# The order of a two-layer graph kernel's transfers: all of one queue in program order, an input loaded into its own tile, additions split and a count moved

## The chip, the cores and the metric

The kernel runs on one core of a Trainium2 chip. The metric is the device time of one execution in microseconds (us), of which the median over several executions is given. Five engines work in parallel, each through its own stream of instructions: TensorE (PE, matrix products into PSUM), VectorE (DVE), ScalarE (ACT), GpSimd (POOL) and SyncE (SP), which here issues nearly all transfers between the memories.

## The reference

For each of 32 items x (512 nodes of 512 features) and one adjacency matrix, two layers are computed, each with its input added back and normalized:

```python
def _L0_gnn_ref(x, adj, Wq, bq, Wk, bk, Wv, bv):
    H, HD = (8, 64)
    q, k, v = ((x @ W + b).reshape(b_, n, H, HD) for W, b in ...)
    scores = einsum('bihd,bjhd->bhij', q, k) / sqrt(HD)
    scores = scores + where(adj == 0, -1e9, 0.0)[None, None, :, :]
    return einsum('bhij,bjhd->bihd', softmax(scores), v).reshape(b_, n, H * HD)

def _L1_gnn_ref(x, adj, weight, bias):
    deg_inv_sqrt = where(adj.sum(1) > 0, rsqrt(adj.sum(1)), 0.0)
    norm_adj = adj * deg_inv_sqrt[:, None] * deg_inv_sqrt[None, :]
    return einsum('nm,bmo->bno', norm_adj, einsum('bni,io->bno', x, weight)) + bias

x = _layernorm(x + _L0_gnn_ref(x, adj, Wq, bq, Wk, bk, Wv, bv))
x = _layernorm(x + _L1_gnn_ref(x, adj, weight, bias))
```

## The kernel before

The items run one after the other in a loop over b (32 of them), with the work of three items interleaved: while attention of item b runs, the keys, queries and values of b + 1 are computed, the graph convolution of b - 1, and the last normalization and the stores of b - 2. An item has two halves. Each half begins with `stretch` (L526) for two of the four groups of heads: scores, exponentials, their sums, and the products with the values. Then follows a run of products on PE, with smaller work of the other engines put at chosen places between them: `play` (L106) takes a list of PE steps and a table "after step n do these". In the first half the PE steps are the keys and queries of b + 1 (L435), in the second the convolution and the values of b + 1 (L379). The products are multiplied out by a seven-product scheme (`seven`, L357), so that PE's steps come in groups of eight matrix products, whose PSUM regions are copied by ACT ("put") or added by DVE ("add"). A region is written again by a later step only when it has been read.

The order on PE, DVE, ACT and POOL is the program's: `InOrder` (L35) wraps these four engines, and each operation goes through `keep_in_program_order` (L45). The transfers issued through SP are not wrapped: `nc.sync.dma_start` leaves it to the framework's scheduler where in SP's stream each is put. SP issues its stream in order. In the program as built, SP's stream in the first item is: eight copies yT<-yb, the store of w1's parts, the load of the values' weights, the store of `fourth`, four copies yT<-yb, two loads of x, four copies, six loads of x, the load of the queries' weights. In later items the four residual loads and the four stores of results stand alternately after the first eight copies yT<-yb, and the x loads stand two before and six after the last four such copies.

The transfers and their tiles:

- `load_x` (L123): x of one item, in two halves of four transfers, rearranged for a transpose by DVE (`turn`, L131; in the trace xT<-e). It fills the last two of the eight buffers of exponentials (`NUM`, in the trace e). In the loop it is called in the second half of item b for item b + 2.
- `load_residual` (L181): x again, in natural order, into the tile xr, for the addition after attention; `gather` (L191), an accumulating transfer that POOL issues, adds the values' bias to it.
- `unload_values` (L507): DVE transposes the product of a head group into yb, a tile with one buffer, and SP copies it in four transfers to yT (L521). The next group's transpose waits for these.
- `swap` (L263): loads the values' weights or the queries' weights, in the form prepared for the seven-product scheme, into one tile wqv that both use in turn.
- `fourth` (L964): in the first item POOL computes one more combination of the values' weights (`weigh_values`), which is stored to the prepared weights in memory (L967). The tile has the tag "lo", one of the places that tiles of several names share one after the other.
- `store` (L840): ACT applies the last normalization, and the result goes out (L850). For most items it lies in the tile y, which has the tag "lo" too, as has `lo` (L677), the low part of the layer's input that DVE computes for the next item.

At the end there is no next item. In the item before the last, the second half's table runs to step 22; then `stretch` of the last item is called with a list `late` to be done between its two groups (L902): the last two `low` and the four `lift` (L682), which add the second layer's bias to yT, on POOL for the item before the last. In the last item's first half the PE steps are the convolution of the item before. After the loop, the last item's own convolution runs alone; `judge` and `count` sum up a check that the fast path was exact (its result decides whether a general version runs), and `measure` takes the statistics for the normalizations.

Of the kernel before, what the change touches and what calls it, by code (L numbers as in the profile page):

```python
# [10 lines left out]
F32 = mybir.dt.float32  # L11
# [7 lines left out]
P = 128  # L19
# [31 lines left out]
def unshifted(  # L51
# [21 lines left out]
    LAST = B - 1  # L73
    tensor, vector, scalar, gpsimd = (InOrder(tc, e) for e in (nc.tensor, nc.vector, nc.scalar, nc.gpsimd))

# [23 lines left out]
    def each(f, *args):  # L99
        return [lambda a=a: f(*a) if isinstance(a, tuple) else f(a) for a in args]  # L100
# [12 lines left out]
    X = {}  # L113
# [8 lines left out]

    def load_x(b, j):  # L123
        X[b, j] = NUM[:, 6 + j].rearrange("p k (n t r) -> p (k n) t r", t=DT, r=32)
        for q in range(4):
            nc.sync.dma_start(
                X[b, j][32 * q : 32 * (q + 1)],
                x[b, ts(j, HALF), ts(q, P)].rearrange("(k s) (t r) -> s k t r", s=32, r=32),
            )
# [51 lines left out]
    def load_residual(b):  # L181
        if b < LAST:
            t = acts.tile([P, NT, D], F32, name="xr", tag="zT", bufs=1)
        else:
            t = wk[:, 3:].rearrange("p k u o -> p k (u o)")
        R[b] = [t[:, i, :] for i in range(NT)]
        for i in range(NT):
            nc.sync.dma_start(R[b][i], x[b, ts(i, P), :])  # L188
        return [lambda: gather(t, rows(bv))]
# [73 lines left out]
    def swap(k):  # L263
        nc.sync.dma_start(wqv, stored[k])
    load_x(1, 0)
# [241 lines left out]
    def unload_values(b, g, av):  # L507
        if b == LAST and g == ORDER[-1]:
            t = work.tile([P, N], F32, name="avT", tag="yb", bufs=1)
            scalar.copy(t[:, :HALF], av[:, :HALF])  # L510
            vector.tensor_copy(t[:, HALF:], av[:, HALF:])
            AV[b, g] = t
            return
        yb = work.tile([P, 4, NT, 32], F32, name="yb", bufs=1)
        vector.transpose(
            yb.rearrange("p l i s -> p i l s"), av.rearrange("p (i r l) -> p i l r", i=NT, l=4)
        )
        if g == ORDER[0]:
            YT[b] = acts.tile([P, NT, D], F32, name="yT")
        for q in range(4):  # L520
            nc.sync.dma_start(  # L521
                YT[b][:, :, (4 * g + q) * 32 : (4 * g + q + 1) * 32],
                yb[32 * q : 32 * (q + 1)],
            )
# [181 lines left out]
    def convolve(b):  # L706
# [135 lines left out]
        def store(n, at):  # L842
            y = row(n)
            rstd, add = (a[:, n - at : n - at + 1] for a in t[at])
            if last and n == 1:
                vector.tensor_scalar(y, y, rstd, add, op0=ALU.mult, op1=ALU.add)
                scalar.dma_start(out[b, ts(n, P), :], y)
                return
            scalar.activation(y, y, AF.Identity, bias=add, scale=rstd)
            nc.sync.dma_start(out[b, ts(n, P), :], y)  # L850

# [43 lines left out]
    for b in range(B):  # L895
# [3 lines left out]
        if b == LAST - 1:  # L899
            nc.sync.dma_start(w1[:, 1:5, 0, P:], stored[2][:, 1:5, 0, P:])  # L900
        biased = []
        late = ahead["low"][2:] + ahead["lift"] if b == LAST else []  # L902
        stretch(b, one, late + back["measure"][:3] if back else ())
# [12 lines left out]
        if b < LAST:  # L916
            k0, k1 = keys_and_queries(b + 1, 0), keys_and_queries(b + 1, 1)
            main = [p for pair in zip(k0, k1) for p in pair]
            if b == 0:
                exact = each(compare, *range(NT))  # L920
                weights = each(lambda k: weigh_part(w1, gpsimd, k), *range(4))
# [17 lines left out]
            if b == 0:  # L939
                nc.sync.dma_start(stored[2], w1)  # L940
        else:
            e = f[b]
            conv = c[b - 1]
            play(conv["first"], {
                0: rest + store[:1] + conv["parts"][:0], 1: store[1:2] + ahead["judge"] + conv["parts"][:1],
                2: store[2:] + e["sums0"],
# [8 lines left out]
        turn0, turn1, combined = turns()  # L955
        if b + 2 < B:
            load_x(b + 2, 0)
            load_x(b + 2, 1)
        if b < LAST:
            end = f[b]  # L960
            if b == 0:
                fourth = acts.tile([P, 4, P], F32, name="fourth", tag="lo", bufs=1)

                def weigh_values():  # L964
                    for k in range(4):
                        weigh_quarter(wqv, wv_quarters, k, gpsimd, fourth)
                    nc.sync.dma_start(stored[1][:, 1:5, 0, P:], fourth)  # L967
                    weigh_quarter(w1, w1_quarters, 3, gpsimd)
# [4 lines left out]
            else:  # L973
# [21 lines left out]
                else:  # L995
# [5 lines left out]
                        15: measure[:1], 16: measure[1:2], 17: measure[2:3], 18: measure[3:] + end["root"],  # L1001
                        19: norm[:1], 20: norm[1:2] + low[:1], 21: norm[2:3] + low[1:2] + biased, 22: norm[3:],
                    }
# [18 lines left out]
    s, tail, halves = e["second"], held["measure"][2:] + held["root"] + held["store"], e["halves"]  # L1022
    run(s[:2] + halves[0] + s[2:4] + end["judge"] + held["measure"][:2])
    vector.tensor_reduce(count, FINE, AX.X, ALU.add)
    run(s[4:5] + tail[:3] + s[5:6])

# [290 lines left out]
```

## Time and profile before

| | us |
|---|---|
| median of 3 runs | 2732.19 (2731.54 to 2735.86) |
| profiled execution, its own time | 2733.05 |
| its span, first to last instruction | 2731.3 |
| mean granted PE clock | 0.996 of full speed |

The profile is that of one execution. In the page's table of transfers (their size in KB, median us from issue to landing) those that the change touches are:

```profile
yT<-yb SPq DMA_DIRECT2D x508, 64.0 KB, 2.4
e<-in_x_dram SPq DMA_DIRECT2D x248, 128.0 KB, 2.6
xr<-in_x_dram SPq DMA_DIRECT2D x122, 256.0 KB, 4.6
...
out_dram<-y SPq DMA_DIRECT2D x120, 256.0 KB, 4.8
```

SPq is SP's queue; x508 is how often. The names are the program's tiles, destination first; e stands for all eight buffers of NUM. Since four engines are wrapped by one helper, the page gives line 45 for almost all of their instructions, and one tells them apart by their tiles. SP's transfers keep their own lines.

### The profile page before, as it was taken

What the parts mean: (1) busy time and instruction counts of PE and PEld (TensorE: products, weight loads), DVE (VectorE), ACT (ScalarE), POOL (GpSimd) and SP (SyncE); (2) the same over time, 40 slices, a digit from 0 to 9 for tenths busy, and PEclk for the clock granted to TensorE, in tenths of its full rate; (3) what the DMA queues carried; (4) which work ended last, traced back from release to release, by engine and by line L of the source; (5) the groups of instructions that cost most, each with busy time, mean ns of one, the idle gap of its engine ahead of it and who ended that gap; (6) DMA issues with size and microseconds to landing.
All of it is one profiled execution on the core that took longest, in us unless ns stands there. A gap on an engine that the chain in (4) does not pass through costs nothing.

```text
span 2731.3 us, 39221 instructions
## 1 busy us (share of the span) xinstructions
PE 2693.9 (99%) x13956; PEld 1913.8 (70%) x13956; DVE 1955.1 (72%) x2743; ACT 1521.9 (56%) x2825; POOL 2051.8 (75%) x1380
## 2 busy tenths in 40 slices
PE   9899999999999999999999999999999999999997
PEld 6576776766767767767667677676676776766764
DVE  4677777677676777776776777777677767777777
ACT  4355555565555655555555556555555555565554
POOL 4577787777887777877778777778777787777764
PEclk9999999999999999999999999999999999999999
DMA  6335444454445454454544454544545444545441
GB/s 186 111 89 135 118 102 130 110 140 124 104 116 130 113 133 116 103 132 110 141 123 106 115 128 117 129 108 107 139 105 147 117 109 115 118 130 128 126 86 49
DMA packets 421996, 324.06 MB, mean 119 GB/s; under 512 B 279840, under 2 KB 348448, under 8 KB 413600
## 3 DMA queue, kind: packets, MB, share of 16 engines
q1 hardware_dynamic: 388048, 255.14, 31.9%
q0 software_dynamic: 32736, 65.02, 15.0%
q8 instruction: 113, 1.85, 0.3%
q10 hardware_dynamic: 1008, 1.31, 0.2%
q14 instruction: 91, 0.75, 0.1%
HBM read 248.78 MB, written 39.32 MB: 105 GB/s over the span
## 4 chain that ended last, share of the span: by engine, by line
PE 89%; POOL 3%; DVE 3%; DMA 2%; SPq 1%; issue 1%; ACT 1%; DVEq 0%; POOLq 0%; ACTq 0%
PE mm L45 58%; PE sc L45 16%; PE av L45 15%; DMA out_dram<-y 2%; POOL yT L45 1%; POOL acc L45 1%; DVE st L45 0%; SPq L188 0%; DVE ve L45 0%; SPq L521 0%; DVE lo L45 0%; DMA yT<-yb 0%; ACT e L45 0%; SPq L850 0%; POOL y L45 0%
## 5 line engine op out<-in xcount | busy, mean ns | idle before, releaser
L45 ACT ACTIVATE e<-e 128x1024 f32<-128x1024 f32 x512 | 540.5, 1057 | 115.9 <-DVE e L45 85.4
L45 POOL TENSOR_TENSOR acc<-acc,e 128x1024 f32<-128x1024 f32 x248 | 588.7, 2374 | 19.4
L45 DVE SCALAR_TENSOR_TENSOR e<-sc,maskT 128x1024 f32<-128x1024 f32 x512 | 585.0, 1214 | 24.0 <-PE sc L45 23.6
L45 PE MATMUL mm<-xT,wk 128*128 128x256 f32 x1792 | 464.3, 381 | 2.4 <-DVE kq L45 2.0
L45 PE MATMUL mm<-xT,wqv 128*128 128x256 f32 x1792 | 459.9, 379 | 0.0
L45 PE MATMUL sc<-kq 64*128 64x512 f32 x2048 | 458.3, 597 | 0.8 <-ACT zT L45 0.8
L45 PE MATMUL av<-e,v 128*64 128x512 f32 x2048 | 453.6, 595 | 0.1
L45 POOL TENSOR_TENSOR xT<-xT 128x512 f32<-128x512 f32 x246 | 327.2, 1340 | 102.9 <-DVE xT L45 70.7
L45 POOL TENSOR_TENSOR acc<-e 128x1024 f32<-128x1024 f32 x126 | 297.0, 2357 | 134.4 <-ACT e L45 134.4
L45 PEld LDWEIGHTS mm<-xT,wk 128*128 128x128 f32 x1792 | 336.6, 190 | 75.9 <-DVE mv L45 23.5
L45 ACT ACTIVATE kq<-mm,bias 128x256 f32<-128x256 f32 x512 | 214.2, 472 | 294.7 <-PE mm L45 288.6
L45 PEld LDWEIGHTS mm<-xT,wqv 128*128 128x128 f32 x1792 | 340.5, 190 | 46.3
L45 POOL TENSOR_TENSOR e<-e 128x512 f32<-128x512 f32 x240 | 303.7, 1276 | 72.5 <-ACT e L45 57.5
L45 PEld LDWEIGHTS sc<-kq 64*128 64x128 f32 x2048 | 192.8, 187 | 234.6 <-issue 177.0
L45 PEld LDWEIGHTS av<-e,v 128*64 128x64 f32 x2048 | 144.7, 137 | 301.4 <-issue 234.4
L45 PE MATMUL mm<-wqv,xT 128*128 128x256 f32 (+1 forms) x1736 | 306.3, 323 | 11.3 <-DVE v L45 11.3
L45 PE MATMUL mm<-w,e 128*128 128x128 f32 (+1 forms) x1680 | 297.9, 323 | 0.2 <-DVE y L45 0.2
L45 PEld LDWEIGHTS mm<-wqv,xT 128*128 128x128 f32 x1736 | 265.1, 192 | 33.6 <-DVE v L45 11.7
L45 DVE STREAM_TRANSPOSE yb<-av 128x512 f32<-128x512 f32 x127 | 91.0, 717 | 273.1 <-DMA yT<-yb 177.1
L45 PEld LDWEIGHTS mm<-w,e 128*128 128x128 f32 x1680 | 253.4, 191 | 25.3 <-DVE y L45 7.5
L45 DVE TENSOR_TENSOR v<-v,mm 128x512 f32<-128x512 f32 x217 | 146.1, 686 | 151.3 <-ACT v L45 76.5
L45 ACT ACTIVATE yT<-yT,inv 128x64 f32<-128x64 f32 x960 | 238.9, 337 | 0.0
(142 smaller groups left out, 3429.9 us busy)
## 6 DMA issues: line engine op xcount, KB each, us to landing
wqv<-wv_parts SPq DMA_DIRECT2D x31, 1792.0 KB, 8.9
wqv<-wq_parts SPq DMA_DIRECT2D x30, 1792.0 KB, 10.2
yT<-yb SPq DMA_DIRECT2D x508, 64.0 KB, 2.4
e<-in_x_dram SPq DMA_DIRECT2D x248, 128.0 KB, 2.6
xr<-in_L_gnn_bv_dram POOLq DMA_DIRECT2D x31, 1024.0 KB, 11.2
xr<-in_x_dram SPq DMA_DIRECT2D x122, 256.0 KB, 4.6
yT<-in_L_gnn_bias_dram POOLq DMA_DIRECT2D x30, 1024.0 KB, 12.3
out_dram<-y SPq DMA_DIRECT2D x120, 256.0 KB, 4.8
```

The source lines that it names most:

```text
L45: return self.tc.keep_in_program_order(op(*args, **kwargs))
```

## The change

Five edits are made together.

1. SP is wrapped like the other engines: all transfers issued through it in the loop, x's, the residual's, the weights', the copies to yT, the stores of results, are issued in the program's order. (In the changed kernel they have line 45 too.)
2. x of the third item (index 2) is loaded in the first half of the first item instead of the second, into a tile of its own, x2, with the tag "lo". `load_x` takes the tile as an argument. The loop's other calls, for later items, stay.
3. `fourth` gets the tag "hi" instead of "lo".
4. Of the four additions of the bias before the last item (`lift`), two move from the gap in the last item's first stretch to the end of the item before, after step 22; the other two move to the last item's first half, after its first step, behind the square roots of the result's normalization.
5. After the loop, the first two measurements of the item before the last come after the check's count and after the fifth step's additions, instead of before the count.

```diff
@@ -71,7 +71,9 @@
     HALF = N // 2
     ORDER = (0, 2, 1, 3)
     LAST = B - 1
-    tensor, vector, scalar, gpsimd = (InOrder(tc, e) for e in (nc.tensor, nc.vector, nc.scalar, nc.gpsimd))
+    tensor, vector, scalar, gpsimd, sync = (
+        InOrder(tc, e) for e in (nc.tensor, nc.vector, nc.scalar, nc.gpsimd, nc.sync)
+    )
 
     consts = ctx.enter_context(tc.tile_pool(name="consts", bufs=1))
     acts = ctx.enter_context(tc.tile_pool(name="acts", bufs=2))
@@ -120,10 +122,11 @@
     def numerators():
         return NUM[:, next(taken) % 8]
 
-    def load_x(b, j):
-        X[b, j] = NUM[:, 6 + j].rearrange("p k (n t r) -> p (k n) t r", t=DT, r=32)
+    def load_x(b, j, t=None):
+        t = NUM[:, 6 + j] if t is None else t[:, j]
+        X[b, j] = t.rearrange("p k (n t r) -> p (k n) t r", t=DT, r=32)
         for q in range(4):
-            nc.sync.dma_start(
+            sync.dma_start(
                 X[b, j][32 * q : 32 * (q + 1)],
                 x[b, ts(j, HALF), ts(q, P)].rearrange("(k s) (t r) -> s k t r", s=32, r=32),
             )
@@ -185,7 +188,7 @@
             t = wk[:, 3:].rearrange("p k u o -> p k (u o)")
         R[b] = [t[:, i, :] for i in range(NT)]
         for i in range(NT):
-            nc.sync.dma_start(R[b][i], x[b, ts(i, P), :])
+            sync.dma_start(R[b][i], x[b, ts(i, P), :])
         return [lambda: gather(t, rows(bv))]
 
     def gather(to, source):
@@ -261,7 +264,7 @@
         engine.tensor_tensor(to, a, c, op)
 
     def swap(k):
-        nc.sync.dma_start(wqv, stored[k])
+        sync.dma_start(wqv, stored[k])
     load_x(1, 0)
     load_x(1, 1)
 
@@ -518,7 +521,7 @@
         if g == ORDER[0]:
             YT[b] = acts.tile([P, NT, D], F32, name="yT")
         for q in range(4):
-            nc.sync.dma_start(
+            sync.dma_start(
                 YT[b][:, :, (4 * g + q) * 32 : (4 * g + q + 1) * 32],
                 yb[32 * q : 32 * (q + 1)],
             )
@@ -847,7 +850,7 @@
                 scalar.dma_start(out[b, ts(n, P), :], y)
                 return
             scalar.activation(y, y, AF.Identity, bias=add, scale=rstd)
-            nc.sync.dma_start(out[b, ts(n, P), :], y)
+            sync.dma_start(out[b, ts(n, P), :], y)
 
         nodes = range(NT)
         leaf, join = quarters_of(left, w1, w1_quarters, lambda: t["whole"], begin, lambda: YT[b])
@@ -897,9 +900,9 @@
         f[b], c[b] = finish(b), convolve(b)
         ahead, back = f.get(b - 1), c.get(b - 2)
         if b == LAST - 1:
-            nc.sync.dma_start(w1[:, 1:5, 0, P:], stored[2][:, 1:5, 0, P:])
+            sync.dma_start(w1[:, 1:5, 0, P:], stored[2][:, 1:5, 0, P:])
         biased = []
-        late = ahead["low"][2:] + ahead["lift"] if b == LAST else []
+        late = ahead["low"][2:] if b == LAST else []
         stretch(b, one, late + back["measure"][:3] if back else ())
 
         def folds(gs):
@@ -917,6 +920,9 @@
             k0, k1 = keys_and_queries(b + 1, 0), keys_and_queries(b + 1, 1)
             main = [p for pair in zip(k0, k1) for p in pair]
             if b == 0:
+                ahead_x = acts.tile([P, 2, 2, N], F32, name="x2", tag="lo", bufs=1)
+                for j in range(2):
+                    load_x(2, j, ahead_x)
                 exact = each(compare, *range(NT))
                 weights = each(lambda k: weigh_part(w1, gpsimd, k), *range(4))
                 beside = {
@@ -937,12 +943,12 @@
                 }
             play(main, beside)
             if b == 0:
-                nc.sync.dma_start(stored[2], w1)
+                sync.dma_start(stored[2], w1)
         else:
             e = f[b]
             conv = c[b - 1]
             play(conv["first"], {
-                0: rest + store[:1] + conv["parts"][:0], 1: store[1:2] + ahead["judge"] + conv["parts"][:1],
+                0: rest + ahead["lift"][:1] + ahead["lift"][3:] + store[:1], 1: store[1:2] + ahead["judge"] + conv["parts"][:1],
                 2: store[2:] + e["sums0"],
                 3: conv["parts"][1:] + e["inverse0"] + ahead["grow"],
             })
@@ -953,18 +959,18 @@
 
         fold0, fold1 = folds(two) if b < LAST else ([], [])
         turn0, turn1, combined = turns()
-        if b + 2 < B:
+        if 0 < b < B - 2:
             load_x(b + 2, 0)
             load_x(b + 2, 1)
         if b < LAST:
             end = f[b]
             if b == 0:
-                fourth = acts.tile([P, 4, P], F32, name="fourth", tag="lo", bufs=1)
+                fourth = acts.tile([P, 4, P], F32, name="fourth", tag="hi", bufs=1)
 
                 def weigh_values():
                     for k in range(4):
                         weigh_quarter(wqv, wv_quarters, k, gpsimd, fourth)
-                    nc.sync.dma_start(stored[1][:, 1:5, 0, P:], fourth)
+                    sync.dma_start(stored[1][:, 1:5, 0, P:], fourth)
                     weigh_quarter(w1, w1_quarters, 3, gpsimd)
 
                 play(values_of(1), {
@@ -999,7 +1005,8 @@
                         1: parts[:1] + fold0 + grow[:2], 2: grow[2:], 3: parts[1:] + fold1, 5: end["inverse"],
                         7: heads[24:] + heads[:6], 11: heads[6:24], 13: end["add"],
                         15: measure[:1], 16: measure[1:2], 17: measure[2:3], 18: measure[3:] + end["root"],
-                        19: norm[:1], 20: norm[1:2] + low[:1], 21: norm[2:3] + low[1:2] + biased, 22: norm[3:],
+                        19: norm[:1], 20: norm[1:2] + low[:1], 21: norm[2:3] + low[1:2] + biased,
+                        22: norm[3:] + end["lift"][1:3],
                     }
                 play(main, beside)
 
@@ -1020,9 +1027,9 @@
     run(block[:1] + norm[3:] + low[2:3] + block[1:2] + low[3:] + block[2:] + end["lift"])
     run(e["unload"] + e["parts"] + [held["extend"][k] for k in (0, 3, 6, 1, 2, 4, 5)] + end["grow"])
     s, tail, halves = e["second"], held["measure"][2:] + held["root"] + held["store"], e["halves"]
-    run(s[:2] + halves[0] + s[2:4] + end["judge"] + held["measure"][:2])
+    run(s[:2] + halves[0] + s[2:4] + end["judge"])
     vector.tensor_reduce(count, FINE, AX.X, ALU.add)
-    run(s[4:5] + tail[:3] + s[5:6])
+    run(s[4:5] + held["measure"][:2] + tail[:3] + s[5:6])
 
     total = P * B * NT * H + N * N + N
     bad = small.tile([1, 1], I32, name="bad")
```

The instructions of PE and ACT and their order are the same in both programs as built. DVE has the same instructions, with two transposes reading x2 instead of e, and the two measurements after the count. POOL has the same, with the additions moved. On SP the transfers are the same in number and size, in the order given in edit 1: in the first item eight copies yT<-yb, eight loads of x2, the store of w1's parts, the values' weights, eight copies yT<-yb, the store of fourth, the queries' weights; in a later item, from its start, eight copies yT<-yb, four stores of y, the values' weights, eight copies yT<-yb, eight loads of x, four residual loads, the queries' weights.

## The prediction

> **What bounds the kernel now.** I read the page first, then TensorE's (PE's) waits, then the timeline around each long one, then the chain of waits in the middle and at the end.
>
> The page's busy line, and the longest entries of PE's waits (waiter, releaser: us in total, times, longest):
>
> ```profile
> PE 2693.9 (99%) x13956; PEld 1913.8 (70%) x13956; DVE 1955.1 (72%) x2743; ACT 1521.9 (56%) x2825; POOL 2051.8 (75%) x1380
> ...
> PE mm L45 <- DVE v L45: 11.3, 1, 11.3
> PE mm L45 <- DMA xr<-in_x_dram: 4.4, 1, 4.4
> PE mm L45 <- DVE kq L45: 2.0, 4, 0.8
> ```
>
> PE sets the time: a change is worth what it takes out of 2731.3 - 2693.9 = 37.4 us of PE idleness, plus matmuls that run at a low clock. The largest wait happens once, and its cause is a queue (timeline: start, length, engine, instruction, and in brackets the idle time before it and what ended it):
>
> ```profile
> 98.86 0.72 DVE L45 STREAM_TRANSPOSE yb<-av 128x512 f32<-128x512 f32 x1 [0.45 <-PE av L45]
> ...
> 102.18 10.63 PE L45 MATMUL mm<-wqv,xT 128*128 128x256 f32 x48
> ...
> 110.97 1.27 POOL L45 TENSOR_TENSOR fourth<-wqv,wv_quarters 128x512 f32<-128x512 f32 x1
> ...
> 112.26 0.37 SPq L967 DMA_DIRECT2D wv_parts<-fourth  x1
> 112.73 2.68 SPq L521 DMA_DIRECT2D yT<-yb  x4
> ...
> 117.33 0.72 DVE L45 STREAM_TRANSPOSE yb<-av 128x512 f32<-128x512 f32 x1 [17.75 <-DMA yT<-yb]
> ...
> 124.08 3.78 PE L45 MATMUL mm<-wqv,xT 128*128 128x256 f32 x8 [11.27 <-DVE v L45]
> ```
>
> The first attention transpose ends at 99.58, but its four copies yT<-yb leave only at 112.73: on SP's queue they stand behind the store of fourth, which GpSimd (POOL) finishes at 112.24. yb has one buffer, so the second transpose waits 17.75 us, the folds and additions to v queue behind it on VectorE (DVE), and PE's last step of the values stands from 112.81 to 124.08.
>
> In the middle, one item as the chain of waits has it:
>
> ```profile
> 1319.64 4.93 POOL yT L45 x4
> ...
> 1324.59 0.35 SPq L188
> ...
> 1327.98 6.49 DMA out_dram<-y
> ...
> 1334.60 0.75 DVE lo L45
> ...
> 1336.01 1.99 PE mm L45 x8
> ```
>
> The result's stores (L850) stand among the residual's loads (L188), which wait for POOL's additions. ScalarE (ACT) had its four y ready at 1320.5, 1321.9, 1323.4 and 1324.8. lo reuses y's memory, so DVE waits for the stores, and its additions to kq queue behind it.
>
> At the end:
>
> ```profile
> 2654.36 5.05 POOL L45 TENSOR_TENSOR yT<-yT,b_r 128x512 f32<-128x512 f32 x4 [0.63 <-DVE lo L45]
> 2658.25 1.18 DVE L45 TENSOR_TENSOR ve<-mv,eps 128x4 f32<-128x4 f32 x1
> 2665.27 6.28 PE L45 MATMUL sc<-kq 64*128 64x512 f32 x28 [0.76 <-ACT zT L45]
> 2714.23 0.19 PE L45 MATMUL mm<-ones,count 128*1 128x1 f32 x2 [1.07 <-DVE count L45]
> 2715.84 0.69 DVE L45 BATCH_NORM_STATS2 st<-y 128x6 f32<-128x512 f32 x1 [0.56 <-POOL y L45]
> ```
>
> A 128x4 operation takes 1.18 us beside POOL's four additions; the same form takes 0.16 at 2717.58. The last two lines: PE waits for the check's count, while DVE's end waits for POOL.
>
> **What the skill says.** The Trainium skill, Perfetto Trace Analysis, DMA Instruction - HWDGE: the issuing sequencer itself waits for an instruction's semaphores before it generates descriptors. The trace agrees: SP issues nothing between the 88.19 swap and 112.26. TensorE: Matmul & The Clock Gate, What's actually happening: after an idle window of about 3.4 us PE runs at half clock until about 3.4 us of work. The trace agrees: the eight matmuls after the wait took 3.78 us, against 10.63/6 = 1.77 for eight before it, at a granted clock of 0.74 from 124.08 to 136.14. SBUF - State Buffer, Who interferes with whom: a DVE operation with two SBUF inputs and a POOL operation that reads SBUF exclude each other. That is the 1.18 above.
>
> **The change part by part.**
>
> *Order of SP.* In the built instruction lists PE and ACT are the same as before. SP now has the program's order: in the first item the values' weights, eight yT copies, then the store of fourth, then the queries' weights; in later items eight yT copies, four stores of y, the values' weights, eight yT copies, eight x loads, four residual loads, the queries' weights.
>
> *Start.* The four copies leave at 99.6 instead of 112.7. From 112.73 to 117.33 they took 4.6 us, so the second transpose runs at 104.2-104.9. Fold one takes 2.4 (to 107.3; POOL's first sum ended at 102.4 at the latest), fold two 2.4 (to 109.8; POOL's second sum ends at 107.2). First addition to v 109.8-110.4. The second needs PE's fifth step, 102.18 + 5 x 1.77 = 111.0, so it ends at 111.7. PE wants it at 112.81: 1.1 us to spare, no wait. Next on DVE is the turn of x, whose eight loads the change puts into the first share: SP issues them at about 69-74 (yT copies until 69.2, then 8 x 0.64), where the DMA share of 60-80 is 0.16; they land 30 us early. The second turn follows PE's last step, 114.6-115.9; the scores' first DVE operation then starts 1.3 us after the scores, as at 89.27 (1.2 after 88.09). PE: eight matmuls 1.77, scores 7.07, attention-values at 112.81 + 1.77 + 7.07 + 0.03 = 121.68 instead of 136.14: **-14.46**. The next run of products took 24.59 against 24.37 elsewhere; I take that 0.22 as the same disturbance: **-0.22**. POOL's combinations of x move with the turns (115.9-121.1) and its sums end 1.1 us later against PE than now; DVE has 151.11 - 148.84 = 2.3 us of cover there (sum ready to its fold). Bounds: no more than 14.7 to gain; if the copies land 3 us late, 2 us of it go. The fourth tile moves to memory last used by the comparison, which DVE ends at 85.1, before POOL's write at 110.97: nothing.
>
> *Middle.* The residual's loads leave the way of the stores: the last store is issued at 1324.8 instead of 1328.0, and with the page's 4.8 us to landing lands at 1329.6, before the 1330.2 at which DVE reaches lo. An undisturbed first half takes 24.37; ten in the chain of waits are longer, by 0.42, 0.67, 0.37, 0.25, 0.10, 0.36, 0.19, 0.36, 0.41 and 1.08, in sum 4.2, and that of the last but one item (2568.30 to 2593.52) by 0.9. All are this wait: **-5.1**. Bounds: 2.0 (what is booked as PE waiting for kq) to 5.1; I take the upper one, since the other first halves show that 24.37 is where PE alone ends.
> What moves back: the x loads follow the second four yT copies (1354.7-1357.4), eight of 0.52 us, so half one lands at 1359.5 + 2.6 = 1362.1 and half two at 1364.2; the turns are at 1371.2 and 1374.0. The residual follows at 1361.7-1363.5 and lands by 1368.1 (4.6); POOL's accumulating transfer starts at 1376.9. Both are covered, by 9 us. The queries' weights wait for PE until 1381 anyway. SP's copies yT in the second half come 0.9 us earlier; nobody waits for them.
>
> *Additions split.* Two of the last item's four go to the end of the item before: POOL is idle for 6.89 us before 2643.94. There the first meets DVE's lo at 2638.88 (0.75), and may hold it by about 0.6; the scores behind have a slack of four PSUM pairs (3.5 us), so nothing. The other two now follow POOL's rstd, so at 2658.25 POOL is idle: ve takes 0.16, ACT's chain up to zT is 1.0 us earlier, and PE's wait of 0.76 goes: **-0.76**. Next late is nothing up to there: PE's own order. Bounds 0 to 0.8.
>
> *Count moved.* The count leaves DVE 1.6 us sooner, two measurements (0.80 each) later. PE's 1.07 goes, but its last product is consumed by DVE at 2720.86, 4.5 us after it ends. DVE does the same work before 2715.84, where POOL's y ends its wait: **0**, bounds -0.5 to +0.5.
>
> Sum: 14.46 + 0.22 + 5.1 + 0.76 = 20.5. Span 2731.3 - 20.5 = 2710.8; the profiled execution's own time 2733.05 - 20.5 = 2712.5; the median of runs, 0.86 lower, 2732.19 - 20.5 = **2711.7**.
>
> **The rivals.** *Start only* : behind lo another wait holds kq (ACT's hi, which five lo already waited for), and the middle keeps its 5.1: 2732.2 - 15.4 = 2716.8. For it: some of those first halves might be limited twice. Against: DVE reaches lo 4.4 us earlier.
> *A late chain at the start*: yb's copies or the folds come later than in the steady items, and PE's last step still waits for v. Each us beyond 1.1 costs one, and beyond about 3.4 the half clock returns (3.0 us): a chain 5 us late gives 2732.2 - 20.5 + 3.9 + 3.0 = 2718.6. Against: each step is taken from a measured twin.
> *The change does nothing*: the yT copies are held by something else too, such as memory of yT: 2732. Against: the transposes before were free to go, and the listed waits of those copies are VectorE and transfer slots.
> *Slower*: the residual's loads, now last in SP's round, land after POOL's accumulating transfer wants them. POOL then holds x's combinations, which PE needs at the next first half, 13 us after they end now. With 8.8 us of cover, PE loses from a landing 22 us later than worked out; 0.95 us in each of 28 items would turn 20.5 gained into 6 lost: 2738.3. For it: all three kinds now lie in one half. Against: the DMA share there is about 0.5.
>
> **How the numbers follow.** All parts 0.75, start only 0.12, late chain 0.06, nothing 0.04, slower 0.03. The range takes the first two with their bounds: from 2708 (0.5 at the end, and 3 for what the middle and end hold that I can't see) to 2717.5. A measurement of this kernel tells 0.2% (5.5 us) from no change: faster 0.93, within 0.04, slower 0.03.
>
> **What would show it.** Right: PE waits for v at the start gone, the second yb transpose at about 104, scores of item two at about 114.6 at full clock; DVE's waits for out_dram<-y (89.0 us, 22 times) gone and every first half at 24.37; no PE wait for zT at the end; the tail from the last product as long as now. Wrong: a PE wait above 2 us anywhere new, POOL waiting for the residual's loads, DVE turns waiting for x, or an item longer than 83.5 us.

## The result, and the profile after

| | before | after |
|---|---|---|
| median (lowest to highest) of 6 runs each | 2735.27 (2731.54 to 2736.66) | 2714.46 (2712.93 to 2716.49) |
| profiled execution, its own time | 2733.05 | 2714.88 |
| its span | 2731.3 | 2712.5 |

The ratio of after to before is 0.9927, with a 95% interval of 0.9914 to 0.994. The forecast was 20.5 us less; the medians differ by 20.8 us and the profiled spans by 18.8. The six runs of before are the three that the forecast started from, with a median of 2732.19, and three more; over all six the median is 2735.27. So a single time of this kernel is good to about 3 us, and that the medians came within 0.3 us of the forecast is in part luck. What follows therefore compares stages inside the profiled executions.

The page's busy line and PE's longest waits after the change (waiter, releaser: us in total, times, longest):

```profile
PE 2688.3 (99%) x13956; PEld 1917.1 (71%) x13956; DVE 1986.2 (73%) x2743; ACT 1522.3 (56%) x2825; POOL 2078.5 (77%) x1380
```

```profile
PE mm L45 <- DMA xr<-in_x_dram: 4.9, 1, 4.9
PE mm L45 <- DVE xT L45: 1.1, 1, 1.1
PE mm L45 <- ACT e L45: 0.7, 1, 0.7
PE mm L45 <- DVE folded L45: 0.6, 1, 0.6
```

PE's wait of 11.3 us for v, the four for kq, the one for zT and the one for the count are gone; that of 0.6 for folded (sums of exponentials that DVE has folded) is new to this list. At the start, the timeline of after:

```profile
99.44 0.72 DVE L45 STREAM_TRANSPOSE yb<-av 128x512 f32<-128x512 f32 x1 [0.45 <-PE av L45]
100.19 8.04 SPq L45 DMA_DIRECT2D yT<-yb  x8
102.77 12.35 PE L45 MATMUL mm<-wqv,xT 128*128 128x256 f32 x56
104.84 0.72 DVE L45 STREAM_TRANSPOSE yb<-av 128x512 f32<-128x512 f32 x1 [4.68 <-PE mm L45]
...
112.38 1.24 DVE L45 STREAM_TRANSPOSE xT<-x 128x1024 f32<-128x1024 f32 x1
112.87 0.38 SPq L45 DMA_DIRECT2D wv_parts<-fourth  x1
...
115.05 7.14 PE L45 MATMUL sc<-kq 64*128 64x512 f32 x32
```

The copies yT<-yb leave right behind the first transpose, the second transpose waits 4.7 us instead of 17.8, PE runs its 56 matmuls without a break, and the store of fourth comes when it can without holding anything. (This execution began 0.6 us later: PE's wait for the very first load was 4.9 instead of 4.4.)

The middle, the item that was shown of before, in three views: DVE's waits for lo, where that for out_dram<-y (89.0 us, 22 times) is no longer among them; the page's row of the stores (the last number is the median us from issue to landing); the timeline:

```profile
DVE lo L45 <- ACT hi L45: 3.7, 4, 1.3
```

```profile
out_dram<-y SPq DMA_DIRECT2D x120, 256.0 KB, 2.0
```

```profile
1304.84 4.98 POOL L45 TENSOR_TENSOR yT<-yT,xr 128x512 f32<-128x512 f32 x4
...
1305.76 4.61 SPq L45 DMA_DIRECT2D out_dram<-y  x4
...
1314.79 0.68 DVE L45 TENSOR_TENSOR kq<-kq,mm 128x512 f32<-128x512 f32 x1
1315.38 0.95 DVE L45 SCALAR_TENSOR_TENSOR lo<-yT,dis,hi 128x512 fp32r<-128x512 f32 x1
```

The four stores no longer wait for POOL's additions: each is issued as soon as ACT has its y ready, the last at 1310.04. The first lo follows its forerunner on DVE at once. It pays for that: it now runs beside POOL's combinations of xT. Of this item's four lo the first three take 0.95, 1.17 and 1.16 us beside them, the last, when POOL has ended, 0.74; POOL's four combinations take 6.04 instead of 5.14. In the list of groups (busy us, mean ns of one, idle time ahead of it), before and after:

```profile
L45 DVE SCALAR_TENSOR_TENSOR lo<-yT,dis,hi 128x512 fp32r<-128x512 f32 x128 | 98.8, 773 | 117.6 <-DMA out_dram<-y 89.0 <-ACT hi L45 22.8 <-ACT yT L45 5.7
```

```profile
L45 DVE SCALAR_TENSOR_TENSOR lo<-yT,dis,hi 128x512 fp32r<-128x512 f32 x128 | 129.9, 1016 | 3.8 <-ACT hi L45 3.7
```

The 114 us of idle time are gone and 31 us of busy time came instead, the whole growth of DVE's busy time on the page (1955.1 to 1986.2). PE waits for none of it. At the end:

```profile
2640.24 0.16 DVE L45 TENSOR_TENSOR ve<-mv,eps 128x4 f32<-128x4 f32 x1
2641.75 2.54 POOL L45 TENSOR_TENSOR yT<-yT,b_r 128x512 f32<-128x512 f32 x2
...
2645.34 7.18 PE L45 MATMUL sc<-kq 64*128 64x512 f32 x32
...
2696.85 0.69 DVE L45 BATCH_NORM_STATS2 st<-y 128x6 f32<-128x512 f32 x1 [0.41 <-POOL y L45]
```

ve takes 0.16 instead of 1.18, and PE's last scores run in one piece.

To see where the time went I divided each execution at the starts of PE's 64 runs of scores (two for each item). An item's first half is the stage from its first run to its second. All us:

```
stage                                   before   after   worked out ahead
before the first scores                  49.43   50.02   -
item 0, 2nd half + item 1, 1st half      79.59   65.12   -14.68
item 1, 2nd half                         44.99   45.44   0
28 first halves (items 2 to 29), above
  38.46 each, in sum                      4.22    0.02   -4.2
item 30, 1st half                        39.34   38.46   -0.9
item 30, 2nd half                        45.78   46.25   0
item 31, 1st half                        24.15   24.32   0
from the last run of scores to the end   67.88   67.17   -0.76
```

Of the stages not listed only one differs by more than 0.06 us: item 3's second half took 45.36 before and 45.01 after, which nothing in the forecast foresaw.

### The profile page after: what moved, and what is told of

It reads as the page before. It is cut to its first block, busy times and chain, and to the rows that moved or that the text cites. A ratio compares the mean times of both kernels' runs of the same rounds, so it can differ in the third digit from the quotient of the medians.

```text
span 2712.5 us, 39096 instructions
## 1 busy us (share of the span) xinstructions
PE 2688.3 (99%) x13956; PEld 1917.1 (71%) x13956; DVE 1986.2 (73%) x2743; ACT 1522.3 (56%) x2825; POOL 2078.5 (77%) x1380
## 5 line engine op out<-in xcount | busy, mean ns | idle before, releaser
L45 POOL TENSOR_TENSOR xT<-xT 128x512 f32<-128x512 f32 x246 | 353.1, 1445 | 90.0 <-DVE xT L45 58.0
```

The source lines that it names most:

```text
L45: return self.tc.keep_in_program_order(op(*args, **kwargs))
```

## The experiments

Each was a kernel of its own. But for the last two, each was run once, and the stages of that profiled execution are compared. The edits are shown in excerpts (... where lines are left out). The single times of before beside them were 2733.98, 2735.78 and 2736.07.

**The order alone.** Edit 1 on the kernel before, nothing else:

```diff
-    tensor, vector, scalar, gpsimd = (InOrder(tc, e) for e in (nc.tensor, nc.vector, nc.scalar, nc.gpsimd))
+    tensor, vector, scalar, gpsimd, sync = (
+        InOrder(tc, e) for e in (nc.tensor, nc.vector, nc.scalar, nc.gpsimd, nc.sync)
+    )
...
-            nc.sync.dma_start(
+            sync.dma_start(
```

> The kernel before with the one edit that SP's transfers are pinned to the program's order. x of the third item is still loaded in the second half of the first item, into the exponentials' buffers. Theory A (the store of fourth held the copies of yb): PE's wait for v at the start (11.3 us) is gone, since the eight copies now leave before that store; x lands at about 112.3 and 114.4 (copies until 107.6, eight loads of 0.52, 2.6 to landing), so its turns are at most 0.6 us late: the two stages from the second score run to the fourth (before 39.70 + 39.89, changed kernel 26.37 + 38.74) come to 65.1 to 65.8 us. Theory B (x had to be loaded early): these two stages stay above 70 us. On both, the first halves of later items are all at 38.46 us, and the end keeps PE's waits of 0.76 for zT and 1.07 for the count. Span on A: changed kernel + 0.8 to + 1.5 us, that is 2713 to 2714.

Measured: 2715.4, span 2713.5. In the timeline the second transpose no longer waits for copies, but the turn of x waits for its loads:

```profile
104.89 0.72 DVE L45 STREAM_TRANSPOSE yb<-av 128x512 f32<-128x512 f32 x1 [4.61 <-PE mm L45]
...
113.75 1.25 DVE L45 STREAM_TRANSPOSE xT<-e 128x1024 f32<-128x1024 f32 x1 [1.18 <-DMA e<-in_x_dram]
```

The double stage (item 0's second half and item 1's first) took 65.50 and every first half 38.46. From the first scores on this kernel is 18.5 us shorter than before, the changed one 19.3. So the order brings nearly everything. It also brings the loss in item 30's second half (46.34, with a wait of 0.7 for folded). PE's waits for zT (0.8) and for the count (1.1) are still there. The double stage is 0.38 us longer than in the changed kernel; the turn's wait for x is the only cause that the trace shows, so this is what edit 2 adds to the order.

**x early, without the order.** Edits 2 and 3 on the kernel before:

```diff
+                ahead_x = acts.tile([P, 2, 2, N], F32, name="x2", tag="lo", bufs=1)
+                for j in range(2):
+                    load_x(2, j, ahead_x)
...
-        if b + 2 < B:
+        if 0 < b < B - 2:
...
-                fourth = acts.tile([P, 4, P], F32, name="fourth", tag="lo", bufs=1)
+                fourth = acts.tile([P, 4, P], F32, name="fourth", tag="hi", bufs=1)
```

> The kernel before with x of the third item loaded in the first half into its own tile and fourth in the other shared place, SP not pinned. In the program as built, the store of fourth then stands ahead of all eight copies of yb. Theory A (the store of fourth held the copies): the wait stays, only the x loads no longer stand among the copies: stages two and three 76 to 79.6 us together, PE waits for v 8 to 11.3 us. Theory B (the early x is what helped): 65 to 67 us, no wait for v. The middle keeps its long first halves (residual loads and stores still alternate): sum of the excess over 38.46 about 5 us on both.

Measured: 2733.82, the double stage 78.83, and the old picture in the timeline:

```profile
111.38 1.27 POOL L45 TENSOR_TENSOR fourth<-wqv,wv_quarters 128x512 f32<-128x512 f32 x1
112.68 0.37 SPq L971 DMA_DIRECT2D wv_parts<-fourth  x1
113.14 7.93 SPq L522 DMA_DIRECT2D yT<-yb  x8
...
117.69 0.72 DVE L45 STREAM_TRANSPOSE yb<-av 128x512 f32<-128x512 f32 x1 [17.71 <-DMA yT<-yb]
```

The scheduler still puts the store ahead of all the copies. The double stage is 0.8 us shorter, but the first halves of the middle are 1.4 us longer in sum than before. Edits 2 and 3 are worth nothing without edit 1.

**Only the one store taken out of the queue.** The kernel before, one line:

```diff
-                    nc.sync.dma_start(stored[1][:, 1:5, 0, P:], fourth)
+                    gpsimd.dma_start(stored[1][:, 1:5, 0, P:], fourth)
```

> The kernel before with one transfer moved: the store of fourth is issued by POOL, not by SP. Nothing else changes, SP is not pinned, x is loaded late. Theory A (that one entry of the queue is the whole hold at the start): PE's wait for v goes, stages two and three come to 65.1 to 66.5 us (x's loads at most 0.5 us late for the turn), and the middle keeps its excess of about 5 us: span 2717 to 2719. Theory B (early x, or the order of the other transfers): the stages stay above 70 us, span above 2724.

Measured: 2718.66, span 2716.9; the double stage 65.12, the middle's excess over 38.46 unchanged at 4.21, item 30's first half 39.26. The timeline of this kernel:

```profile
99.74 2.65 SPq L521 DMA_DIRECT2D yT<-yb  x4
102.32 12.35 PE L45 MATMUL mm<-wqv,xT 128*128 128x256 f32 x56
104.36 0.72 DVE L45 STREAM_TRANSPOSE yb<-av 128x512 f32<-128x512 f32 x1 [4.64 <-PE mm L45]
...
112.71 0.84 POOL L45 DMA_DIRECT2D wv_parts<-fourth  x1 [0.31 <-POOL fourth L45]
```

Nothing else is moved by hand, SP's other transfers follow one another as before (two loads of x still stand between the two groups of copies), and the 14.5 us are there. PE's granted clock is 1.00 from 88 to 130 us. That one entry on SP's queue was the whole loss at the start is hereby shown, wait and low clock together; it also parts the start from the middle.

**The residual's loads ahead of the stores, and right behind them.** Two kernels from the changed one; the loads move from the second half, where both edits take them out, into the first:

```diff
-                    0: rest + scale + ahead["add"], 1: store[:1] + fold0, 2: store[1:2], 3: store[2:3] + fold1,
+                    0: rest + scale + ahead["add"] + loads, 1: store[:1] + fold0, 2: store[1:2], 3: store[2:3] + fold1,
...
```

> The changed kernel with the four residual loads of an item put back into the first half, ahead of the four stores of results, in the pinned order. Theory A (the loads wait for POOL's additions, and the stores stand behind them): DVE's lo waits for out_dram<-y again, about 4 to 6 us in nearly every item, and first halves are long again: excess over 38.46 us of 4 to 10 us in sum, span + 4 to + 10 against the changed kernel. Theory B (the gain in the middle came from elsewhere, such as the earlier copies of yT): first halves stay at 38.46, span within 1 us of the changed kernel.

```diff
-                    4: store[3:] + measure[:2] + (loads if b == LAST - 1 else []), 5: measure[2:] + ahead["root"] + [quarters],
+                    4: store[3:] + measure[:2] + loads, 5: measure[2:] + ahead["root"] + [quarters],
...
```

> After with the residual's four loads issued in the first half behind the four stores instead of in the second half. Order theory (what held lo in the kernel before were stores queued behind the residual's loads and yT's copies on SP): lo waits for no store, all first halves stay 38.46 within 0.1, and b=30's second half is 45.4 to 45.8 as the loads and POOL's accumulating transfers beside yT's copies come at another time. Contention theory (the loads slow the stores wherever they lie near them): DVE's lo waits for out_dram return with 20 us or more in sum, first halves' excess 1 us or more in sum.

Measured, ahead: DVE's lo waits for the stores again,

```profile
DVE lo L45 <- DMA out_dram<-y: 74.0, 23, 4.8
```

and the first halves lose 2.0 us in sum. Behind: no such wait, and nothing lost (0.04). The page's row of the stores tells more than the issue times do. First the kernel with the loads ahead, then that with the loads behind:

```profile
out_dram<-y SPq DMA_DIRECT2D x120, 256.0 KB, 4.9
```

```profile
out_dram<-y SPq DMA_DIRECT2D x120, 256.0 KB, 2.0
```

With four loads of the same size ahead of them on the queue the stores take 4.9 us from issue to landing (4.8 in the kernel before); with the same loads behind them 2.0. The loads behind are near enough to disturb: by the medians over items 2 to 29 all four are issued while the last store is still under way, and it lands in 1.99 us like the others. So the contention theory falls, and what counts is what stands ahead on the queue. One thing is not parted: with the loads ahead, the stores also leave in one burst instead of 1.4 us apart, and a burst alone may cost something, as the four loads that leave together behind the stores land in 2.8, 3.1, 3.6 and 3.9 us.

The expectation of 4 to 10 us was too high: the same wait cost the first halves of the kernel before only 4.2. There the last store landed 3.7 us ahead of the next scores, here 4.1; DVE's wait for the stores is 3.2 us in the mean (74.0 over 23) against 4.0 (89.0 over 22), and only a part of such waits reaches PE.

The 0.8 us which this first kernel (ahead) seemed to gain in item 30's second half (45.44) did not come in the second, and its end stage of 66.69 is no gain in work: the last result but one, which ACT stores itself, is issued 60.3 us after the last scores began, as in the changed kernel, and only SP's last store leaves 0.6 us and lands 0.5 us sooner.

**Edits 4 and 5 undone**, each alone on the changed kernel:

```diff
-        late = ahead["low"][2:] if b == LAST else []
+        late = ahead["low"][2:] + ahead["lift"] if b == LAST else []
...
-                0: rest + ahead["lift"][:1] + ahead["lift"][3:] + store[:1], 1: store[1:2] + ahead["judge"] + conv["parts"][:1],
+                0: rest + store[:1], 1: store[1:2] + ahead["judge"] + conv["parts"][:1],
...
-                        22: norm[3:] + end["lift"][1:3],
+                        22: norm[3:],
```

> After with only the split of the lift's additions undone. Theory A (the split buys 0.8 us at the end by taking zT's additions off the DVE burst, and costs a little in the third-last score run): the PE's wait for zT is back at 0.8, the end stage (from the last score run) 67.6 to 68.0 instead of 67.16, the stage before it 24.13 to 24.15 instead of 24.31, the stage of b=30's second half stays at about 46.25, span 2712.8 to 2713.5. Rival (the split is neutral and the end differs by something else): end stage within 0.2 of 67.16 and no wait for zT.

```diff
-    run(s[:2] + halves[0] + s[2:4] + end["judge"])
+    run(s[:2] + halves[0] + s[2:4] + end["judge"] + held["measure"][:2])
...
-    run(s[4:5] + held["measure"][:2] + tail[:3] + s[5:6])
+    run(s[4:5] + tail[:3] + s[5:6])
```

> After with only the move of the count undone (the two measures again ahead of the count). Theory A (the move costs and brings nothing): span within 0.3 of 2712.5, the DVE's measure waits for POOL's y about 0.5 as before, end stage 67.0 to 67.4. Rival B (the move shortens the tail): end stage 67.6 or more. Rival C (the move lengthens the tail because the measures now come after the count): end stage 66.9 or less.

Measured: without the split, the end takes 68.06 and item 31's first half 24.15 (67.17 and 24.32 with it), and PE's wait is back:

```profile
PE sc L45 <- ACT zT L45: 0.8, 1, 0.8
```

The split brings 0.89 and costs 0.17, net 0.7. The issue of ACT's store, which comes ahead of the last landings and their variation, says the same: 61.3 us after the last scores began without the split, 60.3 with it. With the count back in its place PE waits 1.1 us for it again, the end takes 67.08 and ACT's store is issued at 60.3 as well: edit 5 does nothing to the time.

**The two stages that got longer.** In item 1's second half of the kernel before, POOL's last sum of exponentials reached only into the first of DVE's four scalings of yT. In the changed one the sums start later against DVE's work, since POOL's combinations of x moved with the turns. Before, after, and an experiment in which DVE's first fold (one input an operation) goes ahead of the scaling:

```profile
144.06 4.78 POOL L45 TENSOR_TENSOR acc<-acc,e 128x1024 f32<-128x1024 f32 x2
146.93 4.26 DVE L45 TENSOR_TENSOR yT<-yT,inv 128x512 f32<-128x512 f32 x4
```

```profile
131.28 5.11 POOL L45 TENSOR_TENSOR acc<-acc,e 128x1024 f32<-128x1024 f32 x2
133.02 5.12 DVE L45 TENSOR_TENSOR yT<-yT,inv 128x512 f32<-128x512 f32 x4
```

```diff
-                scale = ahead["inverse"] + ahead["scale"] if b == 1 else []
+                scale = ahead["inverse"] + fold0 + ahead["scale"] if b == 1 else []
...
-                    0: rest + scale + ahead["add"], 1: store[:1] + fold0, 2: store[1:2], 3: store[2:3] + fold1,
+                    0: rest + scale + ahead["add"], 1: store[:1] + (fold0 if b > 1 else []), 2: store[1:2], 3: store[2:3] + fold1,
```

> After with one edit: in the third item's turn, DVE's first fold (a transpose and a reduction of acc, one input each) goes ahead of the four scalings yT<-yT,inv (two inputs from SBUF). Theory A (the scalings take 5.12 instead of 4.26 because POOL's acc sums run beside them, and this is the 0.45 us that item two's second half lost): the scalings take 4.2 to 4.6 us in sum, the score run that followed DVE late is back from 7.52 to 7.1-7.2, the stage 45.44 goes to 45.0-45.1, span 2712.0 to 2712.3. Rival B (DVE is late there for the sum of its work, whatever the order): the scalings get shorter, but something else longer, stage stays 45.3 or more.

```profile
131.75 4.80 POOL L45 TENSOR_TENSOR acc<-acc,e 128x1024 f32<-128x1024 f32 x2
135.75 3.15 DVE L45 TENSOR_TENSOR yT<-yT,inv 128x512 f32<-128x512 f32 x4
...
155.43 9.14 DVE L45 SCALAR_TENSOR_TENSOR e<-sc,maskT 128x1024 f32<-128x1024 f32 x8 [1.21 <-PE sc L45]
```

Taken singly, the scalings beside POOL's sums took 2.45 us before (one), 1.16 and 2.83 in the changed kernel (two), 1.35 in the experiment (one, at the end of the sum); all the others take 0.68. The four take 3.15 us here and the stage is back at 44.98. DVE now waits for PE's scores where it had come late. Theory A holds. (The expected 4.2 to 4.6 was too long: the scaling before was itself disturbed.)

In item 30's second half PE waits 0.57 us for folded. The experiment queues that product one group of matmuls later:

```diff
-                        1: parts[:1] + fold0 + grow[:2], 2: grow[2:], 3: parts[1:] + fold1, 5: end["inverse"],
+                        1: parts[:1] + fold0 + grow[:2], 2: grow[2:], 3: parts[1:] + fold1, 6: end["inverse"],
```

> After with one edit: in b=30's second half the product with folded is queued one group of four matmuls later on the PE. Theory A (the PE waits 0.6 us for folded there, and that wait is the loss of 0.47 in this stage): no wait for folded, stage 61 at 45.6 to 45.8 instead of 46.25, span 2711.8 to 2712.1. Rival B (the wait only moves on, to v or to the inverses' users): stage 61 at 46.1 or more, with another wait in its place.

Measured: no wait for folded, the stage 45.42, lower than expected and lower than in the kernel before (45.78), which had a wait of 0.1 at this product too, though DVE's second transpose waits as long as in the changed kernel (first its line in this kernel, then in after, there with PE's wait):

```profile
2592.41 0.72 DVE L45 STREAM_TRANSPOSE yb<-av 128x512 f32<-128x512 f32 x1 [6.86 <-DMA yT<-yb]
```

```profile
2593.14 0.72 DVE L45 STREAM_TRANSPOSE yb<-av 128x512 f32<-128x512 f32 x1 [6.85 <-DMA yT<-yb]
...
2598.79 0.46 PE L45 MATMUL mm<-folded,spread 128*128 128x128 f32 x2 [0.57 <-DVE folded L45]
```

So the loss arises at that product: up to it the two stages agree to 0.02 us, behind it they differ by 0.83, of which 0.57 is the listed wait. That leaves the transpose, whose lateness makes folded late: its wait was 6.38 before, is 6.85 now, and was 5.88 with the residual's loads ahead of the stores. It waits for four copies yT<-yb, issued 11.5 us after the stage began in all three kernels, and in each the first of these lands 0.3 us behind POOL's accumulating transfer of the second layer's bias, which lands 16.55, 17.04 and 16.08 us after the stage began. So the copies come with this transfer; why it lands half a us later now is not shown.

**The tail.** From 2691 to 2704 DVE is busy nearly without a break, 2.2 us of it with the last item's inverses and the count, beside POOL's additions. The experiment does these two earlier, puts one of POOL's additions ahead of its combinations, and the sixth product's additions ahead of the measurements that wait for POOL:

```diff
-        4: whole[3] + halves[1:] + norm[:1], 5: low[:1] + norm[1:2], 6: low[1:2] + norm[2:3],
+        4: whole[3] + halves[1:] + end["judge"] + [counted] + norm[:1], 5: low[:1] + norm[1:2], 6: low[1:2] + norm[2:3],
...
-    run(e["unload"] + e["parts"] + [held["extend"][k] for k in (0, 3, 6, 1, 2, 4, 5)] + end["grow"])
+    run(held["extend"][:1] + e["unload"] + e["parts"] + [held["extend"][k] for k in (3, 6, 1, 2, 4, 5)] + end["grow"])
...
-    run(s[:2] + halves[0] + s[2:4] + end["judge"])
-    vector.tensor_reduce(count, FINE, AX.X, ALU.add)
-    run(s[4:5] + held["measure"][:2] + tail[:3] + s[5:6])
+    run(s[:2] + halves[0] + s[2:4])
+    run(s[4:5] + held["measure"][:2] + s[5:6] + tail[:3])
```

(`counted` is the reduction to count.)

> After with the tail's DVE and POOL work moved: the last check of the inverses and the count before the last lo's, one of POOL's additions ahead of its last combinations, the product's addition ahead of the last measures. Theory A (behind the last product, DVE is what ends late: it is busy without a break from 2691 to 2704, and 2.2 us of it are the check beside POOL's additions): end stage 65.3 to 66.4 instead of 67.16. Rival B (POOL's last addition to y, done at 2696.8, sets the end): end stage 66.6 to 67.1.

The same operations in after, and in this kernel:

```profile
2691.35 0.60 DVE L45 TENSOR_SCALAR low<-inv 128x32 f32<-128x32 f32 x1
2691.98 1.20 DVE L45 SCALAR_TENSOR_TENSOR low<-inv,low 128x32 f32<-128x32 f32 x1
...
2705.64 0.38 ACTq L45 DMA_DIRECT2D out_dram<-e  x1
```

```profile
2672.19 0.17 DVE L45 TENSOR_SCALAR low<-inv 128x32 f32<-128x32 f32 x1
2672.39 0.19 DVE L45 SCALAR_TENSOR_TENSOR low<-inv,low 128x32 f32<-128x32 f32 x1
...
2703.67 0.39 ACTq L45 DMA_DIRECT2D out_dram<-e  x1
```

Measured: the end stage 65.67, 1.5 us less. ACT's store, the last in these lines, is issued 58.7 us after the last scores began instead of 60.3. Which of the three moves brings how much was not tried apart.

**All three together**, beside the changed kernel once more, five runs of each:

> The three edits fold_first, inverse_later and judge_early together, on the changed kernel. If they add up: the stages 45.0, 45.4 and 65.7 in place of 45.44, 46.25 and 67.16, 2.8 us less than the changed kernel in the same runs, so 0.989 to 0.9925 of the kernel before, span 2709.4 to 2710.0. If one of them only stands in for another (they share no stage, so the profile speaks against it): 1.5 to 2.0 us less.

> The changed kernel once more, for comparison within the same runs: 2712.5 to 2716.5, ratio to before 0.991 to 0.994.

Measured: 2711.61 (2710.87 to 2711.87), ratio to before 0.9916 (0.9903 to 0.993); the changed kernel 2714.37 (2713.14 to 2714.67), ratio 0.9926 (0.9912 to 0.9939). All five runs of the one lie below all five of the other, by 2.8 us in the median; the stages are 45.02, 45.42 and 65.68. The three gains add up.

## Why the prediction was right, and where its sum was off

Faster was right, and 2714.46 lies in the range of 2708 to 2717.5. Against its own reference the span came out at 2712.5 and not 2710.8, 1.7 us of the 20.5 short. The difference is made up of 0.6 for the first load, 0.2 at the start, 0.45 in item 1's second half, 0.47 in item 30's and 0.17 in item 31's first half, less the 0.35 gained in item 3; the rest is spread over many stages. Part by part:

- *Start, -14.46.* The double stage lost 14.47. The one queue entry is shown as the cause by the kernel that moved only that store, and the half clock went with the wait (granted clock 1.00 from 88 to 130 us, against 0.74 from 124 to 136 before). The further -0.22 for the products did not come: item 1's first half still takes 38.74, against 38.46 elsewhere.
- *"DVE has 2.3 us of cover there"* is the step that failed, in the part on the start. I had asked only whether the fold would wait for POOL's sum, and it did not. But the same shift laid more of POOL's sums beside DVE's two-input scalings, and this cost DVE 0.86 us (5.12 against 4.26) and PE 0.45. The Trainium skill, SBUF - State Buffer, Who interferes with whom, which I had used for the end, states the exclusion; the trace agrees here too, with 3.15, 4.26 and 5.12 us for the same four operations.
- *Middle, -5.1.* The first halves lost 4.20 and item 30's 0.88, in sum 5.1. Taking the upper bound was right. The landing time in the working was not: I carried 4.8 us from the page of before, and the stores landed in 2.0 once no loads were ahead of them. It did no harm, as it was on the safe side. (In the item shown the last two stores of before even took 6.3 and 6.5.)
- *"SP's copies yT in the second half come 0.9 us earlier; nobody waits for them"*: in the other items so. In item 30 the copies land 0.5 us later in the stage, PE waits for folded, which stands behind them, and the stage lost 0.47.
- *Additions split, -0.76.* Measured by undoing it: -0.89 at the end. "So nothing" for the scores behind lo was 0.17, net 0.7.
- *Count moved, 0.* Right: 67.08 and 67.17 without and with it. The sign "the tail from the last product as long as now" contradicts this working and did not come: PE ends its last product 2.1 us sooner after the last scores began (50.9 instead of 53.0), the end comes only 0.7 sooner, so the tail grew from 14.9 to 16.3 us.
- *Not in the sum*: 0.6 us are the first load's; PE waited 4.9 us for it instead of 4.4. Over all the profiled executions the first scores began between 48.9 and 50.5 us, before at 49.4 and the changed kernel run again at 49.7: I take it for a variation of that load and no effect of the change.

Of the rivals, "start only" would have left the first halves' 5.1 us in place; they went. "A late chain at the start" would have left PE waiting for v; it does not. "The change does nothing" is refuted by the order alone. For "slower" POOL would have had to wait for the residual's loads; it does not. The sign that I had named beside it, an item longer than 83.5 us, was a poor one: two items are (item 1 with 38.74 + 45.44 = 84.2, item 30 with 38.46 + 46.25 = 84.7), for the two reasons above, and both were longer still before (84.9 and 85.1).

## What to carry to other kernels

When the compute engines have their order written out and the transfers do not, look at the issuing queue first: an entry that waits for a late producer holds all transfers behind it, and a store behind a group of loads can land late even if it is issued in time. When a change moves an engine's work in time, ask what it now lies beside, and not only who waits for its result; of the two small losses here one was shown to be of that kind, the other was a PE wait behind copies that landed later, and each was undone by moving one step. Divide the execution into stages before comparing: 0.45 us in one stage cannot be seen in a time that varies by 3.

## What was not expected of the hardware

The time from issue to landing of the same 256 KB stores was 4.8 to 4.9 us with loads ahead of them on SP's queue and 2.0 with the loads behind. In proportion, small DVE operations suffered most here from work of POOL beside them: the 128x32 operation on low took 1.20 us beside POOL's additions and 0.19 beside a small operation on rstd alone, 1 us that no list of waits shows. The largest case of it is harmless: 31 us in the 128 operations on lo.
